# Constant products in front of a cumulative-sum product, in a two-layer state-space kernel

## The chip, the cores and the metric

The kernel runs on one core of one Trainium2 chip. The metric is the device time of one execution in microseconds (us); three runs of the kernel before gave 20386.96, 20403.19 and 20407.24, so the median is 20403.19.

## The reference, cut to what matters

A network of two "metaformer" layers works on x of shape (8, 128, 64, 64): eight images, 128 channels, 4096 tokens each. Each layer has a token mixer and a feed-forward part. The mixer of the second layer is the one that the change touches. It splits the 128 channels into eight groups of 16 and sends each through a cascade of two small state-space blocks:

```python
def cascade(xi):
    for i in range(cm_in_w.shape[0]):      # two layers
        xi = _mamba(xi, cm_in_w[i], ..., 8, 64)
    return xi
```

The part of such a block that matters here is the decay. A step size dt is a softplus of a projection, A is minus an exponential, and the scan works in chunks on the running sum of dt * A:

```python
dt = jax.nn.softplus(zxbcdt[..., -nh:] + dt_bias)
A = -jnp.exp(A_log)
y = _ssd(xs * dt[..., None], dt * A, Bm, Cm)   # in it: Acs = jnp.cumsum(A, axis=-1)
```

The same layer has a "seed" mixer, a smaller block of the same kind that runs once over all tokens with the batch as its groups.

## The kernel before, in words

The work runs in stages, one after the other, that `run` (line 1676) lists. The first layer's mixer and routing take the first 9800 us. The seed stage (`seeds`, line 1316) runs from about 9800 to 10980 us, the cascade (`cascade`, line 1336) from about 10980 to 18900 us, and the feed-forward part of the second layer (`second_ffn`) from there to the end.

In the cascade an image is cut into 16 segments of 256 tokens, and a segment into two chunks of 128. A segment of a layer passes through `ssd_project` (line 943: the projections, the SiLUs, the step size, the exponents), two times `ssd_chunk` (line 1037: the scan inside a chunk and across chunks) and `ssd_output` (line 1153). These are Python generators. One round of the loop at line 1434 takes the first layer's chunks of segment n, the second layer's chunks of segment n - 2, the projection of the first layer for n + 1 and that of the second layer for n - 1, and the outputs, and weaves them through `until`, `between`, `both` and `slow`. That is the order of the code. The order in which each engine gets its instructions is then made by the scheduler of the build, which may issue an instruction ahead of others when its inputs and its tile are free in its own estimate; in the cascade no order is written out by hand (`self.order` is None there, line 284).

TensorE's results go to PSUM. In the cascade the pool has two tags: "a" with three buffers of two banks (`self.wide`), and "b" with two buffers of one bank (`self.narrow`), 128 partitions by 512 float32 values. All of cs_p, dec_p, cd_p, yo_s_p, y_p and o_p take turns in the two banks of "b".

The names around the change:

- dA (line 1005) is dt * A for a segment, made by a short chain: the raw step size dtr is copied out of tok_p by VectorE (line 990), ScalarE takes absolute value, exponential and logarithm (e_cm, dt_cm), VectorE adds and multiplies (tmp_cm, dt_cm, dA_cm, line 1006).
- cs_p (line 922) is the running sum: one float32 product of dA with the constant triangular matrix "le". The profile shows it as two instructions. It fills 64 partitions by 128 columns of its bank. VectorE splits it into three bfloat16 parts (lines 927 to 930), which go to memory and back in another layout (lines 931 to 940) as ssA and ssB.
- ss_p (line 1075) multiplies ssA and ssB of a segment to get all exponents of a chunk; ScalarE's exponential turns it into E.
- yo_s_p (line 1104) holds what earlier chunks contribute and the new state; VectorE reads it (S_cm and yy_cm).
- y_p (line 1135) gathers the chunk's result: one product with the identity for each half (operands kt and xD_cm), then 64 more with E.
- o_p (line 1167) is the output projection of a segment. In the first layer ScalarE copies it to y1s (line 1387), which is stored and loaded again for the second layer; in the second layer VectorE reads it (ys, line 1393).

The helper `mm` (line 287) issues every product, so that in the profile all of them stand under line 288.

Of the kernel before, what the change touches and what calls it, by code (L numbers as in the profile page):

```python
# [10 lines left out]
BF16 = mybir.dt.bfloat16  # L11
# [12 lines left out]
S = 512  # L24
# [245 lines left out]
def bc(ap, n, axis=None):  # L270

    axis = len(ap.shape) if axis is None else axis
    v = ap.unsqueeze(axis)
    shape = list(v.shape)
    shape[axis] = n
    return v.to_broadcast(shape)


class Net:
# [6 lines left out]

    def mm(self, out, lhsT, rhs, start=True, stop=True):
        self.ordered(self.nc.tensor.matmul(out, lhsT=lhsT, rhs=rhs, start=start, stop=stop))  # L288

    def act(self, out, in_, func, **kw):  # L290
        i = self.ordered(self.nc.scalar.activation(out, in_, func, **kw))  # L291
        if func in (AF.Exp, AF.Ln):
            if self.act_fence is not None:
                self.after(i, self.act_fence)
            self.act_exp = i
        return i
# [557 lines left out]
    def ssd_weights(self, pool, cfg, j):  # L854

        nc = self.nc
        n = f"{cfg.name}{j}"

        def part(i):
            o, m = self.at["stacked"][f"{n}_{i}"]  # L860
            return self.st[:, o : o + m]

        W = pool.tile([128, cfg.cols], F32, name=f"W_{n}")
        nc.vector.memset(W[96:], 0.0)
        self.tt(W[:KST], part(0), part(1), ALU.mult)
        self.tt(W[:KST], W[:KST], part(2), ALU.add)
        negA = pool.tile([128, cfg.nh], F32, name=f"negA_{n}")
        self.act(negA, self.w(f"{n}_Alog"), AF.Exp)
        self.ts(negA, negA, -1.0, ALU.mult)
        D = pool.tile([128, cfg.g2, cfg.nh, cfg.hd], F32, name=f"D_{n}")  # L870
        for g in range(cfg.g2):
            nc.vector.tensor_copy(D[:, g], bc(self.w(f"{n}_D"), cfg.hd))
        wo = pool.tile([cfg.pz, cfg.gh * cfg.co], F32, name=f"wo_{n}")
        self.ts(wo, self.w(f"{n}_out")[: cfg.pz], self.w(f"{n}_rms")[: cfg.pz], ALU.mult)
        return {"W": W, "negA": negA, "D": D.rearrange("p g h q -> p (g h q)"), "wo": wo}

    def ssd_rings(self, pool, cfg, n, npads, nrows, nstates):

# [33 lines left out]
        ring[what] = (q + 1) % len(ring[what + "s"])  # L912
        return ring[what + "s"][q]

    def ssd_exponents(self, cfg, dA, n_tok, ring, wk, ps):


        nc = self.nc
        NC, nh, G = n_tok // 128, cfg.nh, cfg.g
        n = NC * G * nh  # L920
        t_ = cfg.name
        p = ps.tile([128, S], F32, tag="b", bufs=self.narrow, name="cs_p")
        p = p[:n, :128]
        self.mm(p, dA.rearrange("p c g -> p (c g)"), self.k("le"))
        part = wk.tile([n, 3, 128], BF16, name=f"csq_{t_}")
        rest = wk.tile([n, 128], F32, name=f"csr_{t_}")
        nc.vector.tensor_copy(part[:, 0], p)
        self.tt(rest, p, part[:, 0], ALU.subtract)
        nc.vector.tensor_copy(part[:, 1], rest)
        self.tt(part[:, 2], rest, part[:, 1], ALU.subtract)  # L930
        d = self.dp.tile([3, n, 128], BF16, name=f"cs_{t_}", bufs=3)
        nc.sync.dma_start(d.rearrange("i n t -> n i t"), part)
        A, B = self.turn(ring, "row")
        g4 = cfg.g4
        for r in range(g4):
            v = d.rearrange("i (c g h) t -> i c g h t", g=g4, h=nh)[:, :, r]
            nc.sync.dma_start(B[32 * r : 32 * r + 3], v)
            for i in range(3):
                o = 32 * r + 3 + i * nh
                nc.sync.dma_start(A[o : o + nh, :, r], v[i].rearrange("c h t -> h c t"))  # L940
        return A, B, part

    def ssd_project(self, cfg, W, ring, stk, n_tok, wk, ps):
# [3 lines left out]
        nc = self.nc  # L947
# [13 lines left out]
        for j0 in range(0, NP, per):  # L961
            p = ps.tile([128, 2, S], F32, tag="a", bufs=self.wide, name="bc_p")
# [8 lines left out]
        p = ps.tile([128, 2, S], F32, tag="a", bufs=self.wide, name="z_p")  # L971
# [8 lines left out]
        for c in range(NC):  # L980
            p = ps.tile([128, 2, S], F32, tag="a", bufs=self.wide, name="tok_p")
# [15 lines left out]
        def small(name, bufs=2):  # L997
            return wk.tile([128, NC, GH], F32, name=f"{name}_{t_}", bufs=bufs)

        dtr = dtr.rearrange("p c j f -> p c (j f)")  # L1000
        e, r, tmp, dA = (small(n) for n in ("e", "r", "tmp", "dA"))
# [4 lines left out]
        self.tt(dA.rearrange("p c (g h) -> p (c g) h", h=nh), dt.rearrange("p c (g h) -> p (c g) h", h=nh),  # L1006
                bc(W["negA"], NC * G, 1), ALU.mult)
        yield None
        ssA, ssB, part = self.ssd_exponents(cfg, dA, n_tok, ring, wk, ps)
        yield None  # L1010

        p = ps.tile([128, S], F32, tag="b", bufs=self.narrow, name="dec_p")
# [5 lines left out]
        p = ps.tile([128, S], F32, tag="b", bufs=self.narrow, name="cd_p")  # L1018
        n = NC * NP * nh
# [7 lines left out]
        p = ps.tile([128, 2, S], F32, tag="a", bufs=self.wide, name="eA_p")  # L1027
# [648 lines left out]
    def run(self, ctx):  # L1676
        tc, nc, nb = self.tc, self.nc, self.nb
        cp = ctx.enter_context(tc.tile_pool(name="cp", bufs=1))
        dp = ctx.enter_context(tc.tile_pool(name="dp", bufs=1, space=DRAM))
        self.kt = cp.tile(list(self.A["const"].shape), F32, name="kt")  # L1680
        nc.sync.dma_start(self.kt, self.A["const"])
        self.xs = [dp.tile([C, L], F32, name=f"xs_{b}") for b in range(nb)]
        self.ys = [dp.tile([C, L], F32, name=f"ys_{b}") for b in range(nb)]
        self.x1 = [dp.tile([C, L], F32, name=f"x1_{b}") for b in range(nb)]
        self.x2 = [dp.tile([C, L], F32, name=f"x2_{b}") for b in range(nb)]
        self.seed = [dp.tile([C, L], F32, name=f"seed_{b}") for b in range(nb)]
        self.P = [dp.tile([NE, L], F32, name=f"P_{b}") for b in range(nb)]
        self.dp = dp
        self.eo = cp.tile([NE, nb, C], F32, name="eo")
        with tc.tile_pool(name="mid", bufs=1) as mp:  # L1690
            self.pooled = mp.tile([C, NE, nb], F32, name="pooled")
            with tc.tile_pool(name="l0", bufs=1) as pl:
                self.scan_weights(pl)
                self.silus_done([])
                r = pl.tile([C, L], F32, name="r")
                for b in range(nb + 1):
                    with tc.tile_pool(name=f"in{b}", bufs=1) as rp, tc.tile_pool(name=f"inw{b}", bufs=2) as wk, \
                            tc.tile_pool(name=f"inps{b}", bufs=1, space=PSUM) as ps:
                        gens = []
                        if b:  # L1700
                            gens.append(self.route_tokens(b - 1, r, rp, wk, ps))
                        if b < nb:
                            xp, xt = (pl.tile([C, L + 2 * PAD], F32, name=n) for n in ("xp", "xt"))
                            gens.append(self.scan_inputs(b, r, xp, xt, wk, ps))
                        self.turns(*gens)
                    if b < nb:
                        self.first_mixer(b, r, xp, xt)
            self.experts()
        self.act_fence = self.act_exp = None
        pl = ctx.enter_context(tc.tile_pool(name="l1", bufs=1))  # L1710
        self.weights(pl, "second")
        with tc.tile_pool(name="l1s", bufs=1, space=PSUM) as ps:
            self.second_setup(pl, ps)
        self.seeds()
        with tc.tile_pool(name="l1b", bufs=4, space=PSUM) as ps:
            self.gms = pl.tile([C, nb, NSC], F32, name="gms")
            self.wide, self.narrow = 3, 2
            self.cascade(ps)
        self.second_ffn()
# [23 lines left out]
```

## Time and profile before

| what | value |
|---|---|
| median of three runs | 20403.19 us |
| the profiled execution: its span on the page (no other time of it is given) | 20491.5 us |
| mean granted TensorE clock over the span | 0.921 |
| stage 10980 to 18900 us: TensorE busy | 6923.48 of 7920 us |
| the same: VectorE, ScalarE, GpSimd busy | 5290.79, 4654.67, 1531.12 us |
| the same: mean granted clock, share of the DMA engines | 0.94, 0.09 |
| stage 9800 to 10980 us: TensorE busy, granted clock | 958.03 of 1180 us, 0.74 |
| waits of TensorE's cs_p for dA_cm, 11300 to 18650 us | 448.9 us in 239 waits, longest 3.7 us |

How to read it: PE is TensorE's products, PEld its weight loads, DVE VectorE, ACT ScalarE, POOL GpSimd. The granted clock is the share of full speed that TensorE was given by its throttle. A busy time is the union of an engine's instructions; products are pipelined, so two neighbours overlap in it. In the timeline a line gives the start, the time that it covers, the engine, the line of code, the operation, the tiles out<-in, the shape and the count, and in brackets how long the engine was idle before it and which instruction ended that. In the view by stretches of time a line gives the stretch, its length, the busy time of each engine with the count of instructions, the granted clock, the DMA share and GB/s.

### The profile page before, as it was taken

How to read it: one execution, taken by the hardware profiler on the slowest of the kernel's cores; microseconds unless marked ns; L12 is line 12 of the kernel's file. 1: busy time of each engine (PE TensorE's matmuls, PEld its weight loads, DVE VectorE, ACT ScalarE, POOL GpSimd, SP SyncE). 2: the span in 40 equal slices, each digit the busy share in tenths (PEclk: the TensorE clock that was granted, in tenths of full speed). 3: DMA queues.
4: the chain of work that ended last, by engine and by line, in shares of the span. 5: the costliest groups of instructions: out<-in, count | busy, mean ns of one | idle time of the engine just before them, and what ended most of it. 6: DMA issues, size and time to landing. Idle time of an engine off the chain costs nothing. (4 is left out here: it accounts for less than half of the span.)

```text
span 20491.5 us, 295472 instructions
## 1 busy us (share of the span) xinstructions
PE 16535.8 (81%) x111237; PEld 8567.3 (42%) x112221; DVE 15704.4 (77%) x20825; ACT 11194.8 (55%) x15819; POOL 9136.4 (45%) x6292
## 2 busy tenths in 40 slices
PE   7777677777777777777887888888888888888899
PEld 2222222222222222222545666666666666665343
DVE  7989899898989989897354666666666666666886
ACT  5555555555555555554353555555555565555553
POOL 6767577676767767675011112112112112111444
PEclk9989999898999999898687999999999999999899
DMA  4544454454435545444431000000000000001222
GB/s 117 136 106 138 107 136 130 112 135 109 136 108 132 136 109 133 109 132 121 138 124 32 27 26 25 27 25 25 26 26 25 27 26 25 27 25 30 81 97 80
DMA packets 814160, 1684.21 MB, mean 82 GB/s; under 512 B 180859, under 2 KB 413211, under 8 KB 803803
## 3 DMA queue, kind: packets, MB, share of 16 engines
q1 hardware_dynamic: 812734, 1665.25, 29.0%
q8 instruction: 889, 14.57, 0.3%
q14 instruction: 537, 4.40, 0.1%
HBM read 1440.67 MB, written 224.26 MB: 81 GB/s over the span
## 5 line engine op out<-in xcount | busy, mean ns | idle before, releaser
L330 POOL TENSOR_TENSOR bx<-xE,B 128x1024 f32<-128x1024 f32 x2048 | 4819.4, 2354 | 1538.2 <-DMA xE<-dtx_d 1400.7
L288 PE MATMUL dA<-parts,expand 128*128 128x512 bf16 x11816 | 3180.0, 400 | 2124.9 <-DVE last L342 1551.1
L291 ACT ACTIVATE dA<-dA,negA 128x1024 f32<-128x1024 f32 x2048 | 2228.6, 1088 | 3731.3 <-PE dA L288 3647.5
L622 DVE TENSOR_TENSOR_SCAN dA<-dA,last,bx 128x1024 f32<-128x1024 f32 x1536 | 3611.2, 2351 | 209.7 <-POOL bx L330 200.9
L288 PEld LDWEIGHTS <-expand 128*128 128x128 bf16 x12288 | 1078.5, 100 | 4837.7 <-DVE last L342 2739.3
L291 ACT ACTIVATE E_cm<-ss_p 128x1024 f32<-128x1024 f32 x2048 | 1977.1, 1030 | 1545.7 <-PE ss_p L288 674.9
L339 DVE SCALAR_TENSOR_TENSOR E_cm<-E_cm,gm_cm 128x1024 f32<-128x1024 f32 x2048 | 2424.0, 1224 | 512.5 <-ACT E_cm L291 512.1
L330 DVE TENSOR_TENSOR hc<-dA,C 128x1024 f32<-128x1024 f32 x2048 | 2508.0, 1225 | 69.9
L1131 POOL COPY Sd_cm<-S_cm 64x128 f32<-64x128 f32 x1024 | 799.9, 781 | 2886.8 <-DVE S_cm L330 2753.9
L330 POOL TENSOR_TENSOR xD_cm<-tok_cm,D_cm 128x256 f32<-128x256 f32 x512 | 413.8, 808 | 2912.2 <-PE y_p L288 2791.1
L288 PE MATMUL y_p<-E_cm,pad_cm 128*32 128x128 f32 x32768 | 1388.7, 286 | 19.0 <-DVE E_cm L339 10.5
L288 PE MATMUL ss_p<-ssB_cm,ssA_cm 128*128 128x512 bf16 x3584 | 1178.8, 419 | 244.7 <-ACT E_cm L291 167.1
L622 DVE TENSOR_TENSOR_SCAN dA<-dA,bx 128x1024 f32<-128x1024 f32 x512 | 1173.6, 2292 | 197.5 <-POOL bx L330 196.3
L288 PE MATMUL y<-hc,kt 128*32 128x512 f32 x8192 | 1202.0, 652 | 37.8 <-DVE hc L330 31.6
L288 PEld LDWEIGHTS y_p<-E_cm,pad_cm 128*32 128x32 f32 x32768 | 939.4, 113 | 388.6 <-issue 240.7
L288 PE MATMUL bc_p<-stk_cm,W_cm 128*128 128x256 f32 x4096 | 1020.5, 392 | 25.9 <-DMA stk_cm<-xs 20.7
L330 DVE TENSOR_TENSOR gm_cm<-g_p,kt 128x1024 f32<-128x1024 f32 x512 | 624.2, 1219 | 506.3 <-PE g_p L288 501.4
L291 ACT ACTIVATE tok_cm<-tok_p 128x384 f32<-128x384 f32 x1024 | 502.3, 491 | 606.2 <-PE tok_p L288 450.9
L288 PEld LDWEIGHTS bc_p<-stk_cm,W_cm 128*128 128x128 f32 x4096 | 741.0, 191 | 197.0 <-issue 78.8
L291 ACT ACTIVATE BC_cm<-bc_p 128x1024 f32<-128x1024 f32 x512 | 524.9, 1025 | 539.6 <-PE bc_p L288 535.0
L288 PE MATMUL tok_p<-W_cm,stk_cm 128*128 128x200 f32 x4096 | 761.4, 339 | 0.0
L288 PE MATMUL g_p<-BC_cm 64*128 64x128 f32 x8192 | 743.2, 307 | 0.4
(391 smaller groups left out, 30156.3 us busy)
## 6 DMA issues: line engine op xcount, KB each, us to landing
xE<-dtx_d SPq DMA_DIRECT2D x2048, 512.0 KB
dtx_d<-dtx SPq DMA_DIRECT2D x256, 256.0 KB
pb<-p_d SPq DMA_DIRECT2D x64, 1024.0 KB
x<-x SPq DMA_DIRECT2D x192, 256.0 KB
ssA_cm<-cs_cm SPq DMA_DIRECT2D x3072, 4.0 KB
stk_cm<-xs SPq DMA_DIRECT2D x368, 128.0 KB
stk_cm<-y SPq DMA_DIRECT2D x368, 128.0 KB
x<-in_x_dram SPq DMA_DIRECT2D x64, 256.0 KB
```

The lines of the kernel that those rows point to most:

```text
L288: self.ordered(self.nc.tensor.matmul(out, lhsT=lhsT, rhs=rhs, start=start, stop=stop))
L291: i = self.ordered(self.nc.scalar.activation(out, in_, func, **kw))
L330: self.ordered((eng or self.nc.vector).tensor_tensor(out, a, b, op))
L339: self.ordered(self.nc.vector.scalar_tensor_tensor(out=out, in0=a, scalar=s, in1=b, op0=op0, op1=op1))
L622: self.ordered(nc.vector.tensor_tensor_scan(out=t, data0=t, data1=bx.pop(n), initial=0.0 if ch["j"] == 0 else last[:, q : q + 1], op0=ALU. ...
L1131: nc.gpsimd.tensor_copy(Sd[gr, :, g * hi : (g + 1) * hi], S2[gr])
```

## The change: six products into the bank that cs_p overwrites

A tile `warm` of 128 by 512 bfloat16 ones is made once. In `ssd_exponents`, as soon as the bank for cs_p is named and before the product that fills it, `keep_warm` issues `fill` products of that tile with itself (128 by 128 weights, 512 columns) into the whole bank. Nobody reads them: cs_p starts afresh in the part of the bank that is read. `fill` comes from the weights: six where the layer's index j is 0, else none. j is 0 for the first layer of the cascade and for the seed mixer, which has one layer only.

```diff
+    def keep_warm(self, bank, n):
+
+        for _ in range(n):
+            self.mm(bank, self.warm[:, :128], self.warm)
...
-        return {"W": W, "negA": negA, "D": D.rearrange("p g h q -> p (g h q)"), "wo": wo}
+        return {"W": W, "negA": negA, "D": D.rearrange("p g h q -> p (g h q)"), "wo": wo, "fill": 6 if j == 0 else 0}
...
-    def ssd_exponents(self, cfg, dA, n_tok, ring, wk, ps):
+    def ssd_exponents(self, cfg, dA, n_tok, ring, wk, ps, fill):
...
         p = ps.tile([128, S], F32, tag="b", bufs=self.narrow, name="cs_p")
+        self.keep_warm(p, fill)
         p = p[:n, :128]
         self.mm(p, dA.rearrange("p c g -> p (c g)"), self.k("le"))
...
-        ssA, ssB, part = self.ssd_exponents(cfg, dA, n_tok, ring, wk, ps)
+        ssA, ssB, part = self.ssd_exponents(cfg, dA, n_tok, ring, wk, ps, W["fill"])
...
         self.weights(pl, "second")
+        self.warm = pl.tile([128, S], BF16, name="warm")
+        nc.vector.memset(self.warm, 1.0)
```

## The prediction

> **What bounds the kernel now.** I read the page first, for the stage.
>
> ```profile
> span 20491.5 us, 295472 instructions
> PE 16535.8 (81%) x111237; PEld 8567.3 (42%) x112221; DVE 15704.4 (77%) x20825; ACT 11194.8 (55%) x15819; POOL 9136.4 (45%) x6292
> PEclk9989999898999999898687999999999999999899
> ```
>
> TensorE (PE) is busiest, and its clock row never reaches full speed through the right half, which is the cascade (10980 to 18900 us; POOL and DMA are nearly idle there, and by engine TensorE has 6923 of 7920 us). So I asked for single segments: stretches from one first-layer output copy (y1s) to the next, each with the work of one segment of each layer. Columns: stretch, length, busy time of PE, PEld, DVE, ACT, POOL with counts, granted clock, DMA.
>
> ```profile
> 12686.87:12749.60 62.73, 55.55 (x596) 39.31 (x600) 41.49 (x81) 36.42 (x53) 11.74 (x14) 0.92 0.09 25
> 12749.60:12809.69 60.09, 52.73 (x596) 37.42 (x600) 41.49 (x81) 36.46 (x53) 12.18 (x14) 0.97 0.09 26
> 12809.69:12868.67 58.98, 51.48 (x596) 36.90 (x600) 41.56 (x82) 36.35 (x54) 12.19 (x14) 1.00 0.10 27
> ```
>
> The same 596 products take 58.98 us where the clock stays at 1.00, 60.09 at 0.97 and 62.73 at 0.92. That is an experiment that the profile made for us: the clock sets the length of a segment. The first two lengths alternate through most of an image, and full speed is rare. Next, where the clock falls; one segment, TensorE's timeline (start, duration, instruction, count, idle time before and its releaser), then the granted clock around it.
>
> ```profile
> 14039.48 0.63 PE L288 MATMUL o_p<-yz_cm,wo_cm 128*64 128x256 f32 x4
> 14040.47 0.46 PE L288 MATMUL y_p<-kt,xD_cm 128*128 128x128 f32 x2 [0.35 <-DVE yy_cm L330]
> 14043.50 0.66 PE L288 MATMUL cs_p<-kt,dA_cm 128*64 128x128 f32 x2 [2.57 <-DVE dA_cm L330]
> ```
>
> ```profile
> 14038.94:14042.35 3.41, 1.63 (x28) 1.01 (x24) 2.13 (x10) 3.08 (x7) 0.70 (x2) 0.99 0.00 0
> 14042.35:14055.97 13.62, 11.87 (x89) 7.28 (x90) 6.75 (x13) 4.34 (x7) 0.10 (x1) 0.50 0.24 60
> ```
>
> TensorE idles 2.57 us before the first layer's cumulative sum cs_p, because dA comes through the short softplus steps on ACT and DVE. Inside that wait the clock goes to 0.50 and stays there for 13.6 us. Laying the clock record of the cascade beside TensorE's timeline, I find 114 such drops between 11300 and 18650 us, every one at this wait and none at the second layer's (1.2 us idle). They last 1 or 3 units of 3.41 us, mostly, 802 us in all.
>
> [...] only 0.50 and 1.00, lengths in multiples of 3.41. [...] The windows next to this wait give the line: one with 1.63 us of busy time lost the clock (above), one with 1.45 us kept it (below), so the line is near 1.5.
>
> ```profile
> 12810.08:12813.49 3.41, 1.45 (x8) 0.88 (x10) 2.05 (x9) 1.27 (x4) 0.00 (x0) 1.00 0.11 38
> 14040.12:14043.53 3.41, 0.49 (x3) 0.36 (x4) 2.36 (x11) 2.20 (x5) 0.63 (x2) 0.82 0.11 38
> ```
>
> The second line is the emptiest placing of such a window: 0.49 us.
>
> **The change, part by part.** *Price of a product.* ss_p has the same form, 128x128 bf16 weights and 512 columns:
>
> ```profile
> 14024.08 1.02 PE L288 MATMUL ss_p<-ssB_cm,ssA_cm 128*128 128x512 bf16 x4 [0.28 <-ACT E_cm L291]
> 14044.91 1.49 PE L288 MATMUL ss_p<-ssB_cm,ssA_cm 128*128 128x512 bf16 x3 [0.22 <-issue]
> ```
>
> Four take 1.02 us, of which the last one's own length is about 0.38: (1.02 - 0.38) / 3 = 0.213 us apart. At half clock (1.49 - 0.6) / 2 = 0.44. So six take 1.28 us, 2.6 at half clock. Weight loads run beside them.
>
> *Where they run.* They need only the constant tile and the bank. Two banks carry the tag "b"; in TensorE's order the users are yo_s_p, o_p, y_p, cs_p. y_p waited for yo_s_p's reader (yy_cm), so cs_p's bank is o_p's, and o_p's reader is the copy y1s:
>
> ```profile
> 14041.20 0.37 ACT L1387 COPY y1s<-o_p 128x256 f32<-128x256 f32 x1
> 14043.12 0.23 DVE L330 TENSOR_TENSOR dA_cm<-dt_cm,negA_cm 128x64 f32<-128x64 f32 x1
> ```
>
> The bank is free at 14041.57, dA is there at 14043.35: 1.78 us for six products of 1.28 and a semaphore hop (0.15: dA's end to cs_p's start). Cover 0.35 us; cost on the path 0. If they ran at half clock they would push cs_p, and all of TensorE's queue behind it, by 2.6 + 0.15 - 1.78 = 1.0 us, 128 us in all.
>
> *The added wait* for the bank stands at the first of the six; behind it TensorE's queue holds cs_p, which had the same wait, then ss_p and dec_p, which stood behind cs_p anyway. So it adds nothing while the six stay next to cs_p.
>
> *What goes.* The emptiest window rises from 0.49 to 1.77 us, the one that dropped above from 1.63 to 2.3 (0.7 of the six fall into it). That is above the line, though not by much. Without a drop a segment takes 58.98: a pair saves (62.73 - 58.98) + (60.09 - 58.98) = 4.86, 2.43 each. Not all of the 128 gain: five here had no drop, and the eight image starts have a longer wait (3.7 us is the longest) that six do not fill. I take 117: 117 x 2.43 = 284 us. Cross-check: 802 us at half clock is 401 us of lost clock; a segment at 0.92 lost 0.08 x 62.73 = 5.0 and is 3.75 longer, so some 72% counts: 289.
>
> *What is late next* once the drop is gone: what the 58.98 segment shows, TensorE 51.48 busy and the waits for ACT and DVE that are there already.
>
> *The seed stage.* "j == 0" also holds for the seed mixer, so its 16 segments get six products too: 16 x 1.28 = 20 us of TensorE work, in front of a cs_p that waits for dA_sm (69.7 us of idle over 29 waits). Bounds -15 to +20; I take 0. The memset of the constant tile is one DVE instruction once: 0. Everything before 9800 us is unchanged.
>
> *Order.* The build may issue instructions early, so six more of them can shift its order. In the trace ss_p of the second layer stood behind cs_p though it could have run in the wait. Worth -1 to +1 us a segment; I take 0 and keep 128 us both ways as bounds.
>
> The profiled execution has only its span, 20491.5 us, 88 over the median 20403.2 of the runs (0.4%). The sum against it is 20491.5 - 284 = 20207; the same 284 off the median gives **20120 us**.
>
> **The rivals.**
> *A, slower: the six float away.* They are ready long before dA; if they are issued in the first stall with a free bank (say the 1.00 us before ss_p at 14014.16, half a segment earlier) they overrun it by 0.28, hold one of the two banks until cs_p, and the second layer's cs_p must wait for y_p's bank, 0.65 us. The drop stays. (0.28 + 0.65) x 128 = 119, with the lost overlap of dec_p and cd_p perhaps 200: 20520 to 20600. It decides if banks are handed out to whatever is ready first. Against it: at the start of the stage
>
> ```profile
> 11044.86 0.59 PE L288 MATMUL ss_p<-ssB_cm,ssA_cm 128*128 128x512 bf16 x2 [0.32 <-ACT E_cm L291]
> 11050.30 0.47 PE L288 MATMUL cs_p<-kt,dA_cm 128*64 128x128 f32 x1 [4.84 <-DVE dA_cm L330]
> 11050.31 0.47 PE L288 MATMUL yo_s_p<-BC_cm,Sd_cm 128*64 128x128 f32 x1
> ```
>
> yo_s_p had its inputs since about 11022 and both banks were free, yet it stayed behind cs_p through 4.84 us of idle time: it looks as if a tag's banks go in the order of the code. Then the six cannot pass y_p, which is next to cs_p.
>
> *B, no change: the clock drops all the same*[...]; the six hide in the wait: 20400. Half the drops left: 20260.
>
> *C, more: order helps.* The longer stretch before cs_p lets ss_p go ahead of it, 1 us more of the wait is used: 20000.
>
> **How the numbers follow.** Forecast (most drops gone) 0.63, C 0.10, half of the drops left 0.08, B 0.06, A 0.13. The range leaves out the slower half of B, A and the end of C: 20010 to 20390. A measurement of this kernel can tell about 0.2%, 41 us: faster 0.80, same 0.07, slower 0.13.
>
> **What would show it.** Right: in the cascade the granted clock reads 0.99 or 1.00, six products stand just before cs_p with a rest of about 1.2 us of idle time on both sides together, segments of about 59 us, cs_p no later after y1s than 1.9 us. Wrong: the six elsewhere in the order (A); the clock still 0.95 (B); cs_p later by 1 us, the six at 0.43 each; ss_p ahead of cs_p (C).

## The result and the profile after

The changed kernel takes 20122.91 us (median of four runs, 20109.51 to 20168.29); the kernel before took 20401.28 us beside it. The ratio is 0.9872, 95% interval 0.9856 to 0.9888: faster by 278 us. The forecast was 20120.

The profiled execution is the longest of the four (20168.29 us, span 20166.5 us), as that of before was long for its kernel. From the page, the lines that answer those shown of before:

```profile
span 20166.5 us, 298179 instructions
PEclk9989999899999999899686999999999999999899
```

The clock row shows 9 in the cascade, as before: 9 stands for all from 0.90 up, so this row can't tell 0.94 from 1.00, and the prediction read more out of it than it holds ("never reaches full speed"). Single stretches tell it. Columns as before: stretch, length, busy time of PE, PEld, DVE, ACT and POOL, granted clock. Two neighbouring segments, from y1s to y1s, and below them a stretch of 3.41 us around the first layer's wait, placed nearly where it is emptiest:

```profile
12583.46:12642.36 58.90, 53.27 (x606) 37.39 (x606) 41.48 (x81) 36.35 (x53) 12.18 (x14) 1.00 0.10 27
12642.36:12701.26 58.90, 53.27 (x606) 37.39 (x606) 41.48 (x81) 36.35 (x53) 12.18 (x14) 1.00 0.10 27
14120.87:14124.28 3.41, 2.07 (x9) 0.96 (x10) 2.33 (x11) 2.17 (x5) 0.60 (x2) 1.00 0.11 38
```

Before, lengths of 62.73 and 60.09 took turns. Now one segment is like the next, TensorE is busy for 53.27 us instead of 51.48 in the undisturbed one, and the clock reads 1.00. The stretch around the wait has 2.07 us of busy time (2.03 at its emptiest), where the emptiest had 0.49.

TensorE's timeline at the wait, then ScalarE's and VectorE's:

```profile
14121.19 0.46 PE L288 MATMUL y_p<-kt,xD_cm 128*128 128x128 f32 x2 [0.35 <-DVE yy_cm L335]
14122.34 1.46 PE L288 MATMUL cs_p<-warm 128*128 128x512 bf16 x6 [0.69 <-ACT y1s L1393]
14124.12 0.43 PE L288 MATMUL cs_p<-kt,dA_cm 128*64 128x128 f32 x2 [0.33 <-DVE dA_cm L335]
```

```profile
14121.92 0.37 ACT L1393 COPY y1s<-o_p 128x256 f32<-128x256 f32 x1
14123.84 0.22 DVE L335 TENSOR_TENSOR dA_cm<-dt_cm,negA_cm 128x64 f32<-128x64 f32 x1
```

The six stand next to cs_p and are released by y1s, whose bank they take. They end before dA does, and cs_p still waits for dA, the last 0.33 us of it. The wait of 2.57 us has become 0.69 + 0.33 us of idle time with work between.

Where the time went, from the first and last instruction of each stage in the two profiled executions:

| part | before | after | difference |
|---|---|---|---|
| up to the seed mixer's first x_p | 9948.7 | 9910.7 | -38.0 |
| seed stage, first x_p to last det_p | 1029.2 | 1026.5 | -2.7 |
| last det_p to first y1s | 117.9 | 116.3 | -1.6 |
| cascade, first to last y1s | 7766.9 | 7475.6 | -291.3 |
| rest | 1628.7 | 1637.4 | +8.7 |

The first part has the same instructions in every kernel here and lay between 9823 and 9949 us in the profiles of this study, so its 38 us are not the change's. The cascade's 291 us are. In it, counted from the first to the last y1s, 124 clock drops (860 us at 0.50) became 9 (68 us), and of the 127 stretches from y1s to y1s those without a drop rose from 6 to 120; the mean length fell from 61.16 to 58.86 us.

### The profile page after: what moved, and what is told of

The parts are those of the page before. It is cut to its first block, busy times and chain, and to the rows that moved or that the text cites. A ratio compares the mean times of both kernels' runs of the same rounds, so it can differ in the third digit from the quotient of the medians.

```text
span 20166.5 us, 298179 instructions
## 1 busy us (share of the span) xinstructions
PE 16460.5 (82%) x113085; PEld 8450.3 (42%) x113085; DVE 15697.6 (78%) x20826; ACT 11182.7 (55%) x15819; POOL 9162.0 (45%) x6292
## 5 line engine op out<-in xcount | busy, mean ns | idle before, releaser
L288 PE MATMUL y_p<-E_cm,pad_cm 128*32 128x128 f32 x32768 | 1324.3, 278 | 27.6 <-DVE E_cm L344 11.2
L288 PE MATMUL ss_p<-ssB_cm,ssA_cm 128*128 128x512 bf16 x4096 | 1110.3, 384 | 215.3 <-ACT E_cm L296 197.2
L335 DVE TENSOR_TENSOR yy_cm<-yy_cm,y_p 128x256 f32<-128x256 f32 x496 | 207.7, 419 | 665.5 <-PE y_p L288 652.2
```

The costliest lines, as they stand in the source:

```text
L335: self.ordered((eng or self.nc.vector).tensor_tensor(out, a, b, op))
```

## The experiments

The theory: six products keep the busy time of every 3.41 us window above the line at which the clock falls (put near 1.5 us from the trace of before), and that is all they do. Rivals: their presence changes the scheduler's order; it is the length of TensorE's idle time that counts, which the six merely break up; any load at any place would do; the seed stage has a part in it. Each ratio is against runs of the kernel before on the same chip. "Drops" and the lengths are those of the cascade, counted from the clock record and from y1s to y1s; "steady" is the median length of the segments without a drop.

| kernel | ratio, 95% interval | drops | segments of 127 without a drop | mean us | steady us |
|---|---|---|---|---|---|
| before | 1 | 124 | 6 | 61.16 | 58.97 |
| six products (the change) | 0.9872 (0.9856 to 0.9888) | 9 | 120 | 58.86 | 58.90 |
| e1_tiny: six of 8 columns | 0.9978 (0.9969 to 0.9987) | 116 | 14 | 60.92 | 58.91 |
| e2_two | 0.9938 (0.9919 to 0.9957) | 88 | 42 | 60.22 | 58.91 |
| e3_four | 0.9870 (0.9848 to 0.9892) | 29 | 101 | 59.10 | 58.91 |
| e4_ten | 0.9861 (0.9843 to 0.9879) | 4 | 125 | 59.16 | 59.35 |
| e5_second: six, second layer | 0.9977 (0.9965 to 0.9989) | 110 | 19 | 60.84 | 58.87 |
| e6_cascade: six, not in the seeds | 0.9838 (0.9815 to 0.9861) | 10 | 118 | 58.87 | 58.90 |
| e7_zeros | 0.9864 (0.9842 to 0.9886) | 10 | 120 | 58.87 | 58.90 |
| e8_ss_first: no filler, order | 0.9800 (0.9781 to 0.9818) | 58 | 72 | 58.06 | 57.70 |
| e9_six_then_ss | 0.9835 (0.9807 to 0.9863) | 7 | 123 | 58.80 | 58.97 |
| e10_ss_four_ss | 0.9801 (0.9775 to 0.9827) | 12 | 117 | 57.99 | 57.88 |
| e11_seed_ten: seeds only | 0.9995 (0.9985 to 1.0005) | 123 | 7 | 61.15 | 58.97 |
| e12_best: e10 and ten in the seeds | 0.9795 (0.9780 to 0.9810) | 11 | 118 | 57.92 | 57.89 |

**The same instructions with almost no columns.**

```diff
-            self.mm(bank, self.warm[:, :128], self.warm)
+            self.mm(bank[:, :8], self.warm[:, :128], self.warm[:, :8])
```

> The six products keep their number, place, weights and bank, but stream 8 columns in place of 512, so that they keep TensorE busy for a small part of 1.28 us. [...] the drops at the first layer's wait come back: some 110 of them in the cascade, mean granted clock there 0.95, segments of 60.1 and 62.7 us, time 20400 (20340 to 20430). If the gain came from the order of the instructions or from the way the bank is claimed (rival), it stays at about 20123.

Measured: 20339.9 us against 20382.2. TensorE's timeline of e1_tiny at the wait, then two of its segments:

```profile
14157.49 0.29 PE L288 MATMUL cs_p<-warm 128*128 128x8 bf16 x6 [0.69 <-ACT y1s L1393]
14159.27 0.69 PE L288 MATMUL cs_p<-kt,dA_cm 128*64 128x128 f32 x2 [1.49 <-DVE dA_cm L335]
```

```profile
14157.07:14217.17 60.10, 53.56 (x606) 37.69 (x606) 41.60 (x81) 36.48 (x54) 12.20 (x14) 0.97 0.10 26
14217.17:14279.72 62.55, 56.19 (x606) 39.68 (x606) 41.50 (x81) 36.49 (x54) 11.76 (x14) 0.92 0.09 26
```

The six are in the same place, in the same order, with the same wait for y1s, but cover 0.29 us instead of 1.46. The lengths of 60 and 62.5 us are back, and cs_p runs at half clock (0.69 us instead of 0.43). So neither the order nor the wait for the bank is the cause; the busy time is. The six also break up the idle time: its longest piece is 1.49 us now instead of 2.57, and the drops come all the same. A fifth of a per cent is left; in the profiles the cascade is 30 us shorter, with 8 drops fewer.

**Two, four and ten products.**

```diff
-  "fill": 6 if j == 0 else 0
+  "fill": 2 if j == 0 else 0
```

This is e2_two; e3_four has 4 in that place and e4_ten has 10.

> Two products, 0.43 us. Theory, with a line near 1.5 us of busy time in a window of 3.41: the emptiest placing has 0.92, and half of all placings lie under the line (0.75 with none, 0 with six), so about a third of the gain: 20310 (20230 to 20390). Rival (any product in front of cs_p is enough, a matter of order): 20123.

> Four products, 0.85 us: the emptiest placing has 1.35 us, a tenth of all placings lie under 1.5. Theory: nearly the whole gain, 20150 (20115 to 20230), with a few drops left. If the line lay at 1.7, a quarter of the placings would drop: 20220.

> Ten products, 2.13 us, in a wait that holds 1.78 from the free bank to dA. Theory: no drop is left, and cs_p and all behind it come 0.4 to 0.5 us later in each of the 128 segments: 20123 + 60 = 20180 (20140 to 20220). Rival (the products are free as long as TensorE is not the bound): 20123.

Measured: 20247.0, 20108.0 and 20089.1 us against 20382.2. All three are faster than their forecasts, four and ten so much that they lie below their ranges. The stretch of 3.41 us from the end of o_p, close to the emptiest at the wait, holds 1.21 us of busy time with two products (14105.95 to 14109.36), 1.64 with four (14044.95 to 14048.36) and 2.07 with six; the segments with a drop are 85, 26 and 7 of 127. Why does only a part of the segments fall? Two neighbouring segments of e3_four show it, each with a stretch that covers the wait and the one behind it:

```profile
12677.60:12681.02 3.42, 1.96 (x10) 0.73 (x9) 1.99 (x10) 1.49 (x5) 0.00 (x0) 1.00 0.11 38
12681.02:12684.43 3.41, 2.72 (x21) 1.24 (x19) 2.08 (x5) 1.71 (x4) 0.00 (x0) 1.00 0.20 51
12735.63:12739.04 3.41, 1.65 (x8) 0.60 (x6) 2.54 (x12) 2.38 (x5) 0.70 (x2) 1.00 0.12 41
12739.04:12742.46 3.42, 3.37 (x10) 1.58 (x10) 1.69 (x5) 1.10 (x2) 0.00 (x0) 0.50 0.03 6
```

The stretches are not chosen freely. In the cascade of each of the fourteen traces, all changes of the clock lie on one grid of 3.413 us that runs on whatever TensorE does (in that of before 249 changes, none over 1 ns off it); these four are windows of that grid. In the first segment the window holds 1.96 us of busy time and the clock stays, in the second it holds 1.65 and the next window runs at 0.50. Counted over all windows of the grid that ran at full speed, in the fourteen cascades:

| TensorE busy in the window, us | windows | a drop begins at its end |
|---|---|---|
| under 1.30 | 432 | 432 |
| 1.30 to 1.60 | 198 | 176 |
| 1.60 to 1.80 | 164 | 88 |
| 1.80 to 2.20 | 1425 | 15 |
| over 2.20 | 27355 | 0 |

So in these traces the line is near 1.7 us of 3.41, and with two or four products a segment falls or not by where the grid lies in its wait. What decides between 1.3 and 1.8 us I can't say; the profile's busy time is in part modelled. The length of the idle time didn't decide: e2_two is idle for 1.19 us before cs_p and 83 drops begin at that wait (at most 7 of them at the image starts, where it is longer), while none of its drops begins at the second layer's wait of 1.20 us, outside the stage's first two segments and its last.

Ten do cost what was worked out in the cascade:

```profile
14031.46 2.32 PE L288 MATMUL cs_p<-warm 128*128 128x512 bf16 x10 [0.69 <-ACT y1s L1393]
14033.71 0.43 PE L288 MATMUL cs_p<-kt,dA_cm 128*64 128x128 f32 x2
```

```profile
14031.04:14090.39 59.35, 54.18 (x610) 37.96 (x610) 41.60 (x81) 36.38 (x54) 12.20 (x14) 1.00 0.09 27
```

There is no idle time before cs_p any more; it starts 2.67 us after y1s starts instead of 2.20, and the segment is 0.45 us longer. The cascade takes 7513.3 us, 38 more than with six; 60 had been expected. The total doesn't show it: the intervals overlap, and in the profiles the seed stage was 1000.4 us instead of 1026.5. e11_seed_ten looks at that.

**The same six in front of the second layer's sum.**

```diff
-  "fill": 6 if j == 0 else 0
+  "fill": 6 if j == 1 else 0
```

> The same six products, but only in front of the second layer's cumulative-sum product, where the trace of the changed kernel has TensorE idle for 1.20 us and no clock drop begins. Theory (the products pay only where a clock drop would begin): the first layer's wait is bare again, so the drops come back: 105 to 120 of them in the cascade, mean segment 61.1 to 61.4 us, time 20400 (20370 to 20440), where the upper end holds 0.2 us a segment if 1.28 us of work doesn't fit into 1.20 us of wait. Rival (any six products once a segment keep the clock up, because it is the mean load that counts): under 30 drops, segments near 59 us, time near 20125.

Measured: 20405.44 us against 20450.57. TensorE's timeline of e5_second:

```profile
13693.79 1.04 PE L288 MATMUL cs_p<-warm 128*128 128x512 bf16 x4
13694.82 0.59 PE L288 MATMUL ss_p<-ssB_cm,ssA_cm 128*128 128x512 bf16 x2
13695.25 0.59 PE L288 MATMUL cs_p<-warm 128*128 128x512 bf16 x2
...
13702.24 0.43 PE L288 MATMUL cs_p<-kt,dA_cm 128*64 128x128 f32 x2 [1.20 <-DVE dA_cm L335]
```

The 110 drops are there, nearly all still at the first layer's wait, where the same six in front of the first layer's sum left 9. Load elsewhere in the segment didn't help: place matters. But where they run differs from what I had in mind. Here the six did float away, 8.4 us ahead of their cs_p, it seems because their bank was free, and part of them filled TensorE's idle time before an ss_p. They cost nothing (steady 58.87). This kernel is 0.23% below before; in the profiles its cascade is 40 us shorter, with 14 drops fewer, which is about that much. Why fewer began I can't say.

**Without the seed stage, and with zeros.** e6_cascade has the first edit, e7_zeros the second.

```diff
-  "fill": 6 if j == 0 else 0
+  "fill": 6 if j == 0 and cfg is CM else 0
```

```diff
-        nc.vector.memset(self.warm, 1.0)
+        nc.vector.memset(self.warm, 0.0)
```

> The six products only in the cascade's first layer, not in the seed mixer's. Theory (the seed stage gets nothing from them, the whole gain is the cascade's): steady segments 58.90 us, cascade from first to last copy of y1s 7470 to 7490 us, seed stage 1015 to 1035 us as with the products, time within 0.15% of the changed kernel: ratio 0.986 to 0.989. Rival (the products hurt the seed stage, where they stand among other work): seed stage 10 to 20 us shorter, ratio 0.986. Rival (they help there, as the kernel with ten, whose seed stage was 1000 us, made one suspect): seed stage 5 to 15 us longer, ratio 0.988 to 0.9895.

> The constant tile holds 0.0 in place of 1.0, so the six products multiply zeros. Theory (what keeps the clock is that TensorE's columns are running, whatever the numbers): no change from the changed kernel, 12 or so drops in the cascade, segments 58.90 us, ratio 0.986 to 0.989. Rival (it is the switching of the data[...] that the clock follows): the drops of the kernel before come back, ratio 0.995 to 1.0.

Measured: 20135.84 and 20178.14 us against 20450.57. The cascades take 7476.3 and 7477.1 us, with six in both places 7475.6. So the whole gain is the cascade's, and products of zeros keep the clock as well as products of ones (10 drops without the seed stage's six, 10 with zeros, 9 with ones in both places). The seed stage took 1011.3 us without and 1026.1 with the six; kernels without any filler there gave 1011 to 1029, so neither a cost nor a gain of six is established there. The total ratio of e6_cascade was a little below its range; its cascade was not.

**Useful work in the wait instead of filler.** Here cs_p gets an order edge behind the first four ss_p of the second layer (`last` is the ss_p just issued), and there is no filler.

```diff
+        if cfg is CM and st["layer"] == 1 and hf == 0:
+            self.ss_last = last
...
-        self.mm(p, dA..., self.k("le"))
+        cs = self.mm(p, dA..., self.k("le"))
+        if first and self.ss_last is not None:
+            self.after(cs, self.ss_last)
...
-  "fill": 6 if j == 0 else 0
+  "fill": 0
```

> No filler products at all; instead the first layer's cumulative-sum product is ordered behind the four ss_p products of the second layer's first half, which in the changed kernel's trace run just after it (five products in 1.25 us), so that useful work stands in the wait. Theory: about 1.0 us of busy time is added to the emptiest stretch of 3.41 us (0.49 to 1.5 us, at the limit found so far), so half to nine tenths of the drops go: 10 to 60 left in the cascade; the steady segment gains up to 1 us more, because the exponential behind ss_p can start up to 2 us sooner: 58.0 to 58.9 us; time 20150 (20050 to 20270). Rival (the second layer's exponents are not ready that early, or the ScalarE reaches its exponential ahead of the softplus of the first layer and delays dA): cumulative sum later than 2.6 us after y1s, segments 60 us or more, time 20400 to 20550.

Measured: 20059.44 us against 20450.57, more than the six give. TensorE's timeline of e8_ss_first, in which y1s starts at 13429.06:

```profile
13428.63 1.24 PE L288 MATMUL ss_p<-ssB_cm,ssA_cm 128*128 128x512 bf16 x4
13431.22 0.81 PE L288 MATMUL ss_p<-ssB_cm,ssA_cm 128*128 128x512 bf16 x3 [1.35 <-ACT E_cm L296]
13432.48 0.41 PE L288 MATMUL y_p<-E_cm,pad_cm 128*32 128x128 f32 x4 [0.45 <-DVE E_cm L344]
13432.82 0.43 PE L288 MATMUL cs_p<-kt,dA_cm 128*64 128x128 f32 x2
```

The first ss_p don't wait for anything here; they had only stood behind cs_p in the queue. The build went further than the edge: all eight ss_p and some y_p stand ahead of cs_p, which starts 3.76 us after y1s starts, 1.56 later than with six. By the prediction's price of a late cs_p this would cost 1.6 us a segment. Yet the segment is 57.70 us, 1.20 shorter. 58 drops are left, most in the next wait of 1.35 us (the stretch from 13429.80 holds 1.61 us of busy time, again near the line), and they are cheap: segments with one drop average 58.34, 0.64 more than 57.70, where in the kernel before it was 2.3 on average. That is mostly because they are short: 46 of the 58 last one unit of 3.41 us, while before 51 of 124 last three. Among segments from the middle of an image with one drop of one unit, the median is 0.81 over the steady segment here and 1.17 before; a drop of three units cost 3.7 there.

**The six and that order.** The diff is that of e8_ss_first with "fill" at 6 where j is 0.

> The order of the kernel without fillers (cumulative-sum product behind the ss_p products) and the six fillers as well; they stand ahead of ss_p, because they are free to go when y1s has freed their bank. So ss_p starts about 2 us later than without fillers, but about 0.9 us sooner than with the six and the old order, while the cumulative sum comes no sooner than 3.7 us after y1s. Theory (the segment's path runs through ss_p and its exponential, the cumulative sum has slack): under 15 drops, steady segment 58.3 us (57.9 to 58.7), time near ratio 0.983 (0.980 to 0.986). Rival (the path runs through the cumulative sum, as the prediction had it): its delay of 1.5 us or more against 2.20 us shows, segments 60.4 us, ratio 0.994 or above.

Measured: 20095.47 us against 20425.36; the steady segment is 58.97, and neither figure expected for it (58.3 or 60.4) came. The ratio lies in the theory's range, but for its few drops and not for a shorter segment. y1s starts at 18382.22:

```profile
18382.65 1.46 PE L288 MATMUL cs_p<-warm 128*128 128x512 bf16 x5 [0.69 <-ACT y1s L1397]
18383.94 1.24 PE L288 MATMUL ss_p<-ssB_cm,ssA_cm 128*128 128x512 bf16 x5
18387.25 0.43 PE L288 MATMUL cs_p<-kt,dA_cm 128*64 128x128 f32 x2
```

One of the six has no record in this trace, as one of the eight ss_p of e8_ss_first above and one of the first four of e10_ss_four_ss below have none. The events of a segment without a drop, in us from the start of y1s, medians:

| kernel | cs_p | first exponential of ss_p | fourth | segment |
|---|---|---|---|---|
| six products | 2.20 | 3.21 | 7.91 | 58.90 |
| e4_ten | 2.67 | 3.68 | 8.34 | 59.35 |
| e8_ss_first | 3.76 | 1.10 | 4.61 | 57.70 |
| e9_six_then_ss | 5.02 | 2.35 | 5.87 | 58.97 |
| e10_ss_four_ss | 3.76 | 1.10 | 3.81 | 57.88 |

Against e8_ss_first everything in e9_six_then_ss is 1.25 us later, and the segment 1.27 longer: fillers ahead of work that was ready cost their whole length. Against the changed kernel, cs_p is 2.82 us later for only 0.07 us, so cs_p's own time is not the path; but the exponentials 0.9 to 2 us sooner brought nothing either. The time is given back in other waits, as a segment from the middle of an image shows:

```profile
12425.30:12484.27 58.97, 52.56 (x602) 37.43 (x606) 41.11 (x81) 36.47 (x54) 13.08 (x14) 1.00 0.10 27
12443.77 0.65 PE L288 MATMUL o_p<-yz_cm,wo_cm 128*64 128x256 f32 x4 [0.69 <-POOL yz_cm L335]
```

TensorE is idle for 6.41 us in it, in the changed kernel for 5.63. Waits for E, for its masked form and, here, for yz (0.29 us in the changed kernel), all in the first 19 us of the segment, make the difference. What holds those steps back I have not settled.

**Four fillers behind ready work.** The fillers are ordered behind the first four ss_p and ahead of the other four and of y_p, so that they fill the wait of 1.35 us (w is a filler, ss the list of the second layer's ss_p products, ys_in that of its y_p products). They are in the cascade only; the seed mixer has none here.

```diff
+            if first and len(self.ss) >= 8:
+                self.after(w, self.ss[-5])
...
+            self.ss_last = self.ss[-1]
+            for m in self.ss[-4:] + self.ys_in[-16:]:
+                self.after(m, w)
...
+            self.after(cs, self.ss_last)
```

> Four fillers where the order with ss_p ahead still leaves TensorE idle: behind the first four ss_p products and ahead of the other four, which wait 1.35 us for an exponential to free their bank. Theory (the 65 clock drops that are left in the cascade come of that rest; 0.85 us of fillers in 1.35 us of wait delays nothing): 0 to 15 drops in the cascade, steady segment 57.4 to 57.9 us, cascade from first to last copy of y1s 7300 to 7350 us against 7374, ratio 0.977 (0.9755 to 0.979). Rival (the fillers, or the orders that pin them, delay the second four ss_p): steady segment 58.3 us or more, ratio 0.980 to 0.984.

Measured: 20016.26 us against 20425.36. TensorE's timeline of e10_ss_four_ss:

```profile
18276.06 1.03 PE L289 MATMUL ss_p<-ssB_cm,ssA_cm 128*128 128x512 bf16 x3
18276.93 1.03 PE L289 MATMUL cs_p<-warm 128*128 128x512 bf16 x4
18278.65 0.59 PE L289 MATMUL ss_p<-ssB_cm,ssA_cm 128*128 128x512 bf16 x2 [0.27 <-ACT E_cm L297]
```

The fillers delay nothing near them, 58 drops become 12, and the steady segment is in its range. But the mean falls only from 58.06 to 57.99, the cascade takes 7364 us, over the 7350 expected, and the ratio of 0.9801 is over its range too. The gain was small because e8's drops were cheap: 55 segments by 0.64 are 35 us, less 127 by 0.18 for the longer steady segment, leaves 12; 9 were measured.

**Ten in the seed stage alone, and both together.** e11_seed_ten has this edit alone; e12_best is e10_ss_four_ss with ten in the seed mixer as well.

```diff
-  "fill": 6 if j == 0 else 0
+  "fill": 10 if j == 0 and cfg is SM else 0
```

> Ten products in front of the seed mixer's cumulative sum alone, none in the cascade. Theory (the seed stage's clock gains from ten, which is why ten in both places came out no slower than six although its cascade was 38 us longer): seed stage 995 to 1008 us against 1011 to 1029 in the other kernels, cascade as before with 100 to 115 drops, ratio 0.9955 to 0.9985. Rival (the 1000 us there were a lucky profile): seed stage 1011 to 1030 us, ratio 0.997 to 1.0.

> The kernel with four fillers between the two groups of ss_p products, and ten in front of the seed mixer's cumulative sum, which alone took the seed stage to 999 us. Theory (the two gains lie in different stages and add up): steady segment 57.88 us, 12 or so drops in the cascade, seed stage 995 to 1008 us against 1013 without the ten, ratio 0.979 (0.9765 to 0.981). Rival (the seed gain is a matter of the single profile): seed stage 1011 to 1030 us, ratio 0.980 to 0.982.

Measured: 20418.08 us against 20425.36, and 19970.31 against 20385.56. The seed stage, first x_p to last det_p, in e11_seed_ten and in the changed kernel:

```profile
9886.30:10885.70 999.40, 829.12 (x4300) 415.02 (x4316) 527.94 (x1086) 483.94 (x784) 153.73 (x240) 0.80 0.36 114
```

```profile
9910.70:10937.20 1026.50, 845.94 (x4251) 425.29 (x4252) 526.80 (x1086) 484.16 (x784) 153.69 (x240) 0.77 0.35 111
```

The clock is 0.80 against 0.77 and the stage 12 to 30 us shorter than in the kernels without ten there. The three profiles with ten (1000.4, 999.4, 998.6 us) stand apart from the eleven without (1011 to 1029), so the stage gains, and that makes up for most of e4_ten's 38 us. By the whole time it can't be told: e11's interval holds 1, and e12's and e10's overlap. e11's ratio was expected lower, because I took the 0.2% of e1 and e5 for a base, which it isn't.

e12_best is 2.05% faster than before; it, e10_ss_four_ss and e8_ss_first overlap in their intervals, and e8 needs no filler. The intervals of e8 and of the changed kernel do not overlap.

## Why the prediction was right

*Clock drops at the first layer's wait set the segment's length, and busy time decides them.* Right. That the busy time of 3.41 us decides was my inference when it was predicted, from drops in units of 3.41 us and two windows of one trace; the count over all windows shows it. e1_tiny leaves everything but the busy time and loses the gain; e2 to e4 show the dose; e5_second shows that the place must be this wait. Drops also cost what was said: 860 us at half clock made the cascade (61.16 - 58.97) x 127 = 278 us longer, 65% of the 430 us of clock lost, against 72% in the cross-check (its single segment gives 3.75 of 5.0, 75%; with the other of the pair it is 72). The line "near 1.5" was drawn from two windows that a sharp line can't both fit (1.63 us lost the clock, 1.45 kept it); counted over all windows it is near 1.7. Four products, with 1.6 us in the emptiest stretch, were as fast as six within the intervals, with 29 drops left; six stand 0.3 us over the line.

*Price and place of the six.* Right. Their spacing is (1.46 - 0.38) / 5 = 0.216 us against 0.213. They wait for y1s, stand next to cs_p, and cs_p starts 1.83 us after y1s ends, against 1.9 allowed. The idle rest is 1.02 us (1.2 expected). One size was off, and to the good: the emptiest window was to rise to 1.77 us and rose to 2.03. The prediction added 1.28 us, six times the spacing, where six products cover 1.46, because the last one's own length of 0.38 us counts, as its line of four in 1.02 us had shown. At 1.77 the six would have stood barely over the line, so the margin is in part luck. The cover of 0.35 us is real: e4_ten overruns it and pays 0.45 us a segment.

*The sum.* 117 segments by 2.43 us, 284 us; measured 115 drops fewer by 2.53, 291 us in the cascade, and 278 in the medians. At the image starts, where dA comes later (3.6 us after y1s ends), TensorE still idles 2.13 us and the clock still falls at five of the seven that follow the first, as said.

*Seed stage 0.* Within its bounds: -2.7 us between the profiles.

*Order 0.* The order around the change stayed; the rival in which the six float away did not come. e5_second shows that fillers do float where their bank is free, and those, in another place than rival A had in mind (it priced the float at 0.93 us a segment), cost nothing.

*What was right for a wrong reason.* The price of a late cs_p, "and all of TensorE's queue behind it", holds for the order of the changed kernel (e4_ten: 0.47 us later, 0.45 us longer). But the time of cs_p is not what counts in every order: in e8_ss_first it is 1.56 us later and the segment 1.20 shorter, since ready work runs in the wait instead of behind it. What sets the length in general stays open: in e9_six_then_ss the same work runs 0.9 to 2 us sooner than in the changed kernel, and the segment is no shorter. Rival C, ss_p ahead of cs_p for 20000 us, did not happen by itself. With the six kept, as C has it, e9_six_then_ss is that order, and it gives 0.9835, which is 20066 us of 20403: C's price was too good. It is e8_ss_first, without the six, that gives 0.980, 19995 us.

## What to carry to other kernels

Where the granted clock falls at one recurring wait, find the emptiest window there and raise its busy time with enough columns (here from 0.49 to 2.03 us of 3.41), sized to end before the wait does; here six products that nobody reads gave 1.3%. But look first for work in the queue behind the waiting instruction that is ready already: moved ahead it fills the same wait and shortens the segment too, and here gave 2.0% without any filler. Where both are used, put the fillers behind the ready work: ahead of it, in e9_six_then_ss, they cost 1.27 us a segment, their whole length, and behind it, in e10_ss_four_ss, 0.18.

## What the runs showed of the hardware

- In these fourteen cascades the clock changed only on a grid of 3.413 us, and whether it dropped went with the busy time in the grid's window that just ended: under 1.30 us all of 432 windows were followed by half clock, over 2.20 us none of 27355; between 1.60 and 1.80 us 88 of 164 were.
- It didn't take one long idle time: in before the wait of 2.57 us had a drop, and in e8_ss_first one of 1.35 us with short work around it (1.61 us busy in 3.41) still had most of the 58 drops.
- What the running columns carried made no difference: zeros kept the clock as ones did (10 drops in e7_zeros and in e6_cascade, 58.90 us in both).
- Six products of 8 columns, 0.29 us in all, left 116 of 124 drops; six of 512 columns, 1.46 us in all, left 9.
- A drop cost more the longer it lasted: one unit of 3.41 us cost 1.17 us of a segment and three cost 3.7 in the kernel before; in e8_ss_first one unit cost 0.81.
